# Four heads in one tile: exponentials, adds and masks of an attention step on Trainium2

## The chip, the cores and the metric

The kernel runs on one core of one Trainium2 chip. A core has five engines that run side by side, each with its own queue of instructions: TensorE (PE, matrix products; PEld are its weight loads), VectorE (DVE), ScalarE (ACT), GpSimd (POOL) and SyncE (SP), which here only issues transfers. PE writes to PSUM; the other data lie in SBUF, and the inputs and outputs in HBM. Instructions wait for each other by semaphores.

The metric is the device time of one execution in microseconds (us). Before the change it is 2343.66 us, the median of three runs (2343.58 to 2346.75).

## The reference, cut to what matters

The program computes one transformer block with conditioning, on x of 2 x 2048 x 512 in float32: 16 heads of 32, causal attention, and an MLP of 2048.

```
qkv = (xm @ Wqkv) -> q, k, v            # 2 batches, 16 heads, 2048 tokens, 32 per head
scores = q k^T * hd ** -0.5, causal     # each query sees itself and what is before it
attn = softmax(scores)
out = attn v -> x + gate * (out @ Wproj + bproj)
h = gelu(norm(x) @ W1 + b1);  x + gate * (h @ W2 + b2)
```

The change lies in the softmax: the exponentials, their causal mask, and the sums over the keys by which the output is divided.

## The kernel before, in words

The block is computed in stages: the products for q, k and v of a batch, the attention of that batch (`attention_phase`, once for each batch), its projection, and the MLP at the end. The change touches `attention_phase` alone. In the profile it runs from about 210 to 745 us and from about 982 to 1518 us.

**Units and steps.** Heads go in groups of four (HC = 4), which fill the 128 partitions of a product's output. A unit is one group c (four of them) with one block i of 512 queries (four of them): 16 units to a batch, numbered u, in the order i = 0, 1, 2, 3 for the first group and 0, 2, 1, 3 for the others. A unit goes over its keys in steps of 128 keys: 4i steps with all 512 queries, then three steps at the diagonal. The first of these (step 4i) has one block of 128 x 128 on the diagonal at its start; the second (step 4i + 1, the "two-block step") holds two key tiles of 384 and 128 queries in one bank, so it has two diagonal blocks; the last has 256 queries and one diagonal block. A batch has 144 steps, the kernel 288.

**One step** (`scores_t`): for each of the four heads PE writes the scores of 128 keys by up to 512 queries into a PSUM bank `st` (first a product that subtracts each query's maximum, L614, then the scores, L622); ACT writes the exponentials to a tile `e` of SBUF (L630), one of 128 x 512 for each head; at the diagonal POOL sets what lies above the diagonal to zero with `affine_select` (L636), one for each head, which covers one or two blocks. Between the heads PE and DVE compute the row maxima of later units (`row.score`, L500 and L495).

**Two steps later** (LAG = 2) PE multiplies the values by the exponentials (`values`, `products`, tile `o`). The products of a two-block step are done tile by tile: the 384 queries of all four heads, then the 128 of all four.

**The sums over the keys** are products with ones (`row_sums`, tile `sm`). To make fewer of them, the exponentials of up to four full steps are first added elementwise into a tile `ee` for each head: `begin_chain` adds the first two steps, `add_to` each later one (L658), and the diagonal step 4i is added to the last chain. POOL does these adds, except in a batch's last unit (u = 15), where DVE does them. The product with ones follows four steps after the chain's last add was issued.

**Buffers.** `e` has 16 buffers of one head, that is four steps; `ee` has 8, that is two chains. An exponential waits until everything that reads the buffer's old content is done.

**Order.** Each engine works through its own instructions in the order in which the program issues them; `act` and `mm` keep that order. So a select stands in POOL's queue behind all adds issued before it. In the last unit `row.prepare` (L446) adds work for the projection: products of two SBUF tiles on DVE (L459, L467) and an add on POOL (L465). After a batch's last unit its sums go to HBM (`finish`, L684), are read back (`load_sums`, L373), inverted on DVE (L380), written and read again; POOL multiplies the attention's result by them (tile `at`, L1266), and PE projects it (`ps_o`). In that stretch SP also loads pieces of the MLP's weights (L1154), which POOL adds up (L1166).

Of the kernel before, what the change touches and what calls it, by code (L numbers as in the profile page):

```python
# [8 lines left out]
F32 = mybir.dt.float32  # L9
F32R = mybir.dt.float32r  # L10
BF16 = mybir.dt.bfloat16
AF = mybir.ActivationFunctionType
ALU = mybir.AluOpType
# [4 lines left out]
P = 128  # L18
# [3 lines left out]
QB = 512  # L22
# [5 lines left out]
def dit_block_kernel(  # L28
# [36 lines left out]
    nc = tc.nc  # L65
# [5 lines left out]
    HC = P // HD  # L71
    TQ = QB // P
# [1 line left out]
    MTT = MT // P  # L74
    NG = T // MT
    LAG = 2
    E_BUFS = 16
    EE_BUFS = 8
    AHEAD = 3

    const = ctx.enter_context(tc.tile_pool(name="const", bufs=1))
# [53 lines left out]
    first = const.tile([P, 1], F32, tag="first", name="first")  # L135
# [68 lines left out]
    def mm(*args, **kw):  # L204

        return tc.keep_in_program_order(nc.tensor.matmul(*args, **kw))  # L206

    def act(ins):

        return tc.keep_in_program_order(ins)  # L210
# [70 lines left out]
    units = []  # L281
# [298 lines left out]
    def attention_phase(row):  # L580
        b, vv, kst, qst = row.b, row.vv, row.kst, row.qst
        with pool(f"att{b}") as ap, pool(
# [6 lines left out]
            def scores_t(u, step, n):  # L589

                def st_bank():

                    n_bank[0] += u == len(units) - 1
                    if n_bank[0] % 6 >= HC:
                        return ps_sp.tile([P, QB], F32, tag="s", name="st")
                    return ps_stp.tile([P, QB], F32, tag="st", name="st")

                c, i = units[u]
                tiles = steps_of[u][step]
                q0 = tiles[0][1]
                w = sum(QB - q for _, q in tiles)
                sts, es = [], []  # L610
                for h in range(HC):
                    g = slice(h * HD, (h + 1) * HD)
                    st = st_bank()
                    mm(  # L614
                        st[:, :w], sel[g, :], fold[u % 2][g, q0 : q0 + w],
                        start=True, stop=False,
                    )
                    sts.append(st)
                for h in range(HC):
                    at = 0  # L620
                    for j, q in tiles:
                        mm(  # L622
                            sts[h][:, at : at + QB - q],
                            kst[c, j // TQ][:, h, j % TQ * P : (j % TQ + 1) * P],
                            qst[u][:, h, q:],
                            start=False, stop=at + QB - q == w,
                        )
                        at += QB - q
                    e = ap.tile([P, QB], F32, tag="e", name="e", bufs=E_BUFS)
                    act(nc.scalar.activation(e[:, :w], sts[h][:, :w], AF.Exp))  # L630
                    if tiles[0][0] >= i * TQ:

                        d = e.rearrange("p (t k) -> p t k", k=P)[:, 0 : TQ : TQ - 1, :]
                        d = d[:, : len(tiles), :]
                        act(
                            nc.gpsimd.affine_select(  # L636
                                d, d, pattern=[[0, len(tiles)], [1, P]],
                                compare_op=ALU.is_ge, fill=0.0,
                                base=0, channel_multiplier=-1,
                            )  # L640
                        )
                    es.append(e)
                    if h < 2 and n >= 3 or h >= HC - n and n < 3:
                        row.score(1)
                if n >= 3:
                    row.score(1, st_bank)
                    row.score(min(n, HC) - 3)
                return es, max(0, n - HC)

            def new_sums():  # L650
                return [
                    ap.tile([P, QB], F32, tag="ee", name="ee", bufs=EE_BUFS)
                    for _ in range(HC)
                ]

            def add(u, h, dst, x, y):
                engine = nc.vector if u == len(units) - 1 else nc.gpsimd
                act(engine.tensor_tensor(dst, x, y, ALU.add))  # L658

            def add_to(u, chain, es):  # L660
                for h in range(HC):
                    add(u, h, chain[h], chain[h], es[h])

            def begin_chain(u, es0, es1):
                chain = new_sums()
                for h in range(HC):
                    add(u, h, chain[h], es0[h], es1[h])
                return chain

            def products(dst, lhs, es, q0, at, first, last):  # L670
                for h in range(HC):
                    mm(
                        dst[h * HD : (h + 1) * HD, q0:], lhs(h),
                        es[h][:, at : at + QB - q0], start=first, stop=last,
                    )

            def finish(u, o, sm):
# [26 lines left out]
            for u, (c, i) in enumerate(units):  # L704
                for n, tiles in enumerate(steps_of[u]):
                    w = sum(QB - q for _, q in tiles)
# [3 lines left out]
            def due(u, step):  # L710

                rate, past = 0.0, weight[step]
                for v in range(u + 1, len(units)):

                    left = sum(weight[step : max(step + 1, starts[v] - 3)])
                    rate = max(rate, (cum[v] - row.spent) / left)
                return row.spent + rate * past

            for u, (c, i) in enumerate(units):
# [5 lines left out]
                for n_step, tiles in enumerate(steps_of[u]):  # L725
                    last = n_step == steps - 1
                    if n_step == 0:
# [5 lines left out]
                    n = row.count(  # L733
                        due(u, starts[u] + n_step) - QB // 2,
                        u + AHEAD - (n_step < 2 and u > 0),
                    )
                    if u == 0 and n_step < LAG:

                        n = max(n, HC)
                    es, rest = scores_t(u, n_step, n)  # L740
                    rest = len(row.todo) - rest
                    make_rows = False
# [14 lines left out]
                    def tile_by_tile(dst, lhs, es, tiles, first, last):  # L757
                        at = 0
                        for n, (j, q) in enumerate(tiles):
                            products(  # L760
                                dst, lambda h: lhs(j, h), es, q, at,
                                first and n == 0, last and n == len(tiles) - 1,
                            )
                            at += QB - q
# [15 lines left out]
                    if n_step < i * TQ:  # L780
                        k = n_step % TQ
                        if k == 0:
                            even = es
                        elif k == 1:
                            chain = begin_chain(u, even, es)
                        else:
                            add_to(u, chain, es)
                        if k == TQ - 1 and n_step + 1 < i * TQ:
                            sums_of, wait = (chain, False), 2
                    elif i and n_step == i * TQ:  # L790
                        add_to(u, chain, es)
                        sums_of, wait = (chain, False), 2
                    else:

                        sums_of, wait = (es, last, tiles), i > 0 and not last
# [478 lines left out]
    row = Row(0)  # L1274
    with pool("wada") as wp, pool("qkv0") as qp, pool("hl0") as hp, pool(
# [161 lines left out]
        pieces.done()  # L1437

    attention_phase(row)


    past, row = row, Row(1)
    with pool("qkv1") as qp, pool("ps_qkv1", bufs=6, space=PSUM) as ps_mm:
# [29 lines left out]
        with pool("hl1") as hp:  # L1473
# [17 lines left out]
            pieces.done()  # L1491

    attention_phase(row)
    ps_s_cm.__exit__(None, None, None)

# [541 lines left out]
```

## Time and profile before

| | |
|---|---|
| median of three runs | 2343.66 us (2343.58 to 2346.75) |
| the profiled execution | 2339.57 us |
| its span, first to last instruction | 2337.8 us |
| granted TensorE clock | 0.997 of full speed |
| instructions | 34364 |

How to read the lines that follow. The page gives the busy time of each engine with its share of the span and its count of instructions; then digits for 40 equal slices of the span, each the busy share of a slice in tenths; then the chain of work that ended last, in shares by engine. A line of the view of waits reads: who waited, for whom, us in total, how often, longest us. A line of the timeline reads: start in us, length in us, engine, source line, operation, tile written <- tiles read, shapes, how many such instructions are merged in it, and in brackets the engine's idle time before it and what ended that. A group reads: line, engine, operation, tiles, shapes, count, busy us and mean ns of one, idle us before it. A line that lists a source's instructions gives min/median/max ns. The ends of matmuls are modelled, so PE looks somewhat busier than it is.

### The profile page before, as it was taken

To read this page: it belongs to the slowest core of one execution; us is meant where nothing else is said; L and a number is where in the kernel's file an instruction comes from. 1 tells how busy PE (TensorE), PEld (TensorE's weight loads), DVE (VectorE), ACT (ScalarE), POOL (GpSimd) and SP (SyncE) were. 2 spreads that over 40 slices of the span, in tenths; PEclk is the share of its full clock that TensorE was granted. 3 is DMA by queue.
4 is the path that set the end of the run, shared out by engine and by line. 5 is a ranking of instruction groups with operands and counts; after the bars stand their busy time and mean duration, and the time that the engine had idled before them with its cause. 6 is when DMAs were issued, how large, how long until landed. Compare 5 with 4: busy or idle time off the path is not lost.

```text
span 2337.8 us, 34364 instructions
## 1 busy us (share of the span) xinstructions
PE 2272.5 (97%) x12033; PEld 1376.1 (59%) x12033; DVE 1432.3 (61%) x3025; ACT 1007.9 (43%) x1952; POOL 1119.2 (48%) x1261
## 2 busy tenths in 40 slices
PE   7999999999999999999999999999999999999998
PEld 5787445455544588754545554344585486487477
DVE  4677766767657657777576766562473383375356
ACT  4434555555555243355555555603323322332320
POOL 7153997988893692289888898450000000000000
PEclk9999999999999999999999999999999999999999
DMA  9887132231223796622324113263354254353433
GB/s 303 272 277 185 33 86 65 64 83 46 91 100 116 260 307 222 167 60 67 75 64 100 42 42 133 97 229 108 107 176 154 84 176 145 116 162 126 141 120 131
DMA packets 160518, 311.64 MB, mean 133 GB/s; under 512 B 16544, under 2 KB 48844, under 8 KB 158552
## 3 DMA queue, kind: packets, MB, share of 16 engines
q1 hardware_dynamic: 155488, 285.53, 40.5%
q0 software_dynamic: 4480, 23.36, 2.6%
q8 instruction: 95, 1.56, 0.3%
q14 instruction: 79, 0.65, 0.1%
q10 hardware_dynamic: 376, 0.55, 0.1%
HBM read 229.95 MB, written 87.29 MB: 136 GB/s over the span
## 4 chain that ended last, share of the span: by engine, by line
PE 83%; DVE 6%; POOL 6%; issue 2%; DMA 2%; ACT 1%; SPq 0%; DVEq 0%; POOLq 0%; ACTq 0%
PE ps_a L206 24%; PE st L206 15%; PE ps_b L206 12%; PE o L206 9%; PE s L206 7%; PE ps_c L206 6%; POOL ee L658 5%; PE sm L206 4%; PE ps_o L206 3%; DVE junk L495 2%; PE ps_xt L214 1%; DVE mx L500 1%; POOL e L636 1%; ACT e L630 1%; PE ps_o L214 1%
## 5 line engine op out<-in xcount | busy, mean ns | idle before, releaser
L630 ACT ACTIVATE e<-st 128x512 f32<-128x512 f32 (+1 forms) x1152 | 574.5, 578 | 413.6 <-PE st L206 380.0
L500 DVE TENSOR_REDUCE mx<-s 128x1 f32<-128x512 f32 x608 | 406.2, 686 | 223.1 <-PE s L206 221.8
L658 POOL TENSOR_TENSOR ee<-ee,e 128x512 f32<-128x512 f32 x424 | 529.1, 1293 | 3.5 <-ACT e L630 3.3
L206 PE MATMUL st<-qst,kst 128*128 128x512 f32 (+3 forms) x1280 | 410.6, 386 | 0.0
L206 PE MATMUL s<-kst,qst 128*128 128x512 f32 (+3 forms) x994 | 375.3, 402 | 6.0 <-DVE mx L500 3.1
L206 PE MATMUL ps_a<-sum,w 128*128 128x256 f32 (+1 forms) x1088 | 346.6, 454 | 0.0
L206 PE MATMUL o<-e,vv 128*32 128x512 f32 (+3 forms) x2560 | 310.2, 539 | 6.9 <-POOL e L636 6.7
L206 PEld LDWEIGHTS st<-qst,kst 128*128 128x128 f32 x1280 | 227.8, 188 | 117.6 <-issue 88.3
L206 PEld LDWEIGHTS ps_a<-sum,w 128*128 128x128 f32 x1088 | 206.4, 190 | 109.7 <-issue 91.3
L658 POOL TENSOR_TENSOR ee<-e 128x512 f32<-128x512 f32 x168 | 210.3, 1288 | 102.3 <-ACT e L630 100.6
L495 DVE CUSTOM_DVE_ANT_0 junk<-s,causal 128x128 bf16<-128x128 f32 (+3 forms) x386 | 188.5, 488 | 92.4 <-PE s L206 85.0
L206 PEld LDWEIGHTS s<-kst,qst 128*128 128x128 f32 x994 | 185.7, 188 | 55.5 <-DVE mx L500 20.5
L636 POOL TENSOR_SCALAR_AFFINE_SELECT e<-e 128x128 f32<-128x128 f32 (+1 forms) x384 | 123.6, 362 | 73.1 <-ACT e L630 70.8
L206 PEld LDWEIGHTS <-sel 32*128 32x128 bf16 x1152 | 29.5, 91 | 199.7 <-issue 199.7
L1616 DVE TENSOR_TENSOR h<-c,ps_b 128x512 f32<-128x512 f32 x32 | 22.0, 688 | 202.0 <-PE ps_b L206 202.0
L206 PE MATMUL st<-fold,sel 32*128 32x512 bf16 (+1 forms) x1152 | 127.9, 372 | 13.5 <-DVE mx L495 6.4
L206 PEld LDWEIGHTS o<-e,vv 128*32 128x32 f32 x2560 | 65.3, 108 | 112.4 <-issue 72.8
L1790 ACT ACTIVATE h<-h,cols 128x512 f32<-128x512 f32 x96 | 69.3, 722 | 120.5 <-DVE h L1616 120.5
L206 PE MATMUL ps_b<-sum,w 128*128 128x256 f32 (+1 forms) x384 | 120.6, 450 | 0.0
L500 DVE TENSOR_REDUCE mx<-st 128x1 f32<-128x512 f32 x160 | 109.4, 684 | 2.4 <-PE st L206 0.6
L985 POOL TENSOR_TENSOR lo<-lo,hi 128x512 fp32r<-128x512 f32 x32 | 40.7, 1274 | 130.4 <-ACT hi L983 124.1
L206 PE MATMUL st<-kst,qst 128*128 128x512 f32 (+3 forms) x286 | 98.0, 370 | 0.0
(210 smaller groups left out, 3113.9 us busy)
## 6 DMA issues: line engine op xcount, KB each, us to landing
kst<-k SPq DMA_DIRECT2D x128, 256.0 KB
qst<-q SPq DMA_DIRECT2D x128, 256.0 KB
w<-w1d SPq DMA_DIRECT2D x32, 896.0 KB
w<-w2d SPq DMA_DIRECT2D x28, 1024.0 KB
w<-w2d SPq DMA_DIRECT2D x28, 768.0 KB
q<-hi SPq DMA_DIRECT2D x32, 256.0 KB
q<-lo SPq DMA_DIRECT2D x32, 256.0 KB
k<-hi SPq DMA_DIRECT2D x32, 256.0 KB
```

The source lines that it names most:

```text
L206: return tc.keep_in_program_order(nc.tensor.matmul(*args, **kw))
L214: return tc.keep_in_program_order(nc.tensor.transpose(dst, src, ident[:n, :n]))
L495: nc.vector.tensor_tensor_reduce(junk[:, :w], x, causal[:, QB - w :], 1.0, MASKED, ALU.add, ALU.max, m,)
L500: nc.vector.tensor_reduce(m, x, axis=AX.X, op=ALU.max)
L630: act(nc.scalar.activation(e[:, :w], sts[h][:, :w], AF.Exp))
L636: nc.gpsimd.affine_select(d, d, pattern=[[0, len(tiles)], [1, P]], compare_op=ALU.is_ge, fill=0.0, base=0, channel_multiplier=-1,)
L658: act(engine.tensor_tensor(dst, x, y, ALU.add))
L985: engine.tensor_tensor(lo, d, hi.bitcast(F32), ALU.subtract)
L1616: act(nc.vector.tensor_tensor(dst, x, y, ALU.add))
L1790: nc.scalar.activation(d, ps, AF.Gelu, bias=col(r_b1 + half * HF + f, 1))
```

## The change

The four heads of a step share one tile `e` of 128 x 4 x 512, and the four heads of a chain one tile `ee` of that size. There are 4 and 2 buffers of them, the same memory as before. ACT still writes one exponential for each head. POOL adds all four heads in one operation of 128 x 2048. The selects of a step come after its four exponentials, one for each diagonal block with the four heads in it: one in a one-block step, two in a two-block step. DVE's adds in the last unit stay one for each head. Products read the head's part of the tile. In the built program the order of the instructions on PE and ACT is the same as before. On DVE one operation of the projection between the batches changes place with its neighbours. In SP's queue transfers change places in the projections behind each attention phase: behind the first, loads of weight pieces for the MLP (L1154) now stand after the results of the last unit (`finish`, L684 and L685), some of them after the loads of x too; behind the second, loads of x, stores of x1 and loads of the MLP's weights are interleaved in another way. Only the first exponential of a step waits for the tile `e` to come free, and it waits for the whole add of the step that held it before.

```diff
-    E_BUFS = 16
-    EE_BUFS = 8
+    E_BUFS = 4
+    EE_BUFS = 2
...
+                e4 = ap.tile([P, HC, QB], F32, tag="e", name="e", bufs=E_BUFS)
                 for h in range(HC):
...
-                    e = ap.tile([P, QB], F32, tag="e", name="e", bufs=E_BUFS)
-                    act(nc.scalar.activation(e[:, :w], sts[h][:, :w], AF.Exp))
-                    if tiles[0][0] >= i * TQ:
-
-                        d = e.rearrange("p (t k) -> p t k", k=P)[:, 0 : TQ : TQ - 1, :]
-                        d = d[:, : len(tiles), :]
+                    act(nc.scalar.activation(e4[:, h, :w], sts[h][:, :w], AF.Exp))
+                    if h < 2 and n >= 3 or h >= HC - n and n < 3:
+                        row.score(1)
+                if tiles[0][0] >= i * TQ:
+                    for n_t in range(len(tiles)):
+                        lo = n_t * (TQ - 1) * P
+                        d = e4[:, :, lo : lo + P]
                         act(
                             nc.gpsimd.affine_select(
-                                d, d, pattern=[[0, len(tiles)], [1, P]],
+                                d, d, pattern=[[0, HC], [1, P]],
                                 compare_op=ALU.is_ge, fill=0.0,
                                 base=0, channel_multiplier=-1,
                             )
                         )
-                    es.append(e)
-                    if h < 2 and n >= 3 or h >= HC - n and n < 3:
-                        row.score(1)
...
-            def add(u, h, dst, x, y):
-                engine = nc.vector if u == len(units) - 1 else nc.gpsimd
-                act(engine.tensor_tensor(dst, x, y, ALU.add))
+            def add(u, dst, x, y):
+                if u < len(units) - 1:
+                    act(nc.gpsimd.tensor_tensor(dst, x, y, ALU.add))
+                    return
+                for h in range(HC):
+                    act(nc.vector.tensor_tensor(dst[:, h], x[:, h], y[:, h], ALU.add))
 
             def add_to(u, chain, es):
-                for h in range(HC):
-                    add(u, h, chain[h], chain[h], es[h])
+                add(u, chain, chain, es)
 
             def begin_chain(u, es0, es1):
-                chain = new_sums()
-                for h in range(HC):
-                    add(u, h, chain[h], es0[h], es1[h])
+                chain = ap.tile([P, HC, QB], F32, tag="ee", name="ee", bufs=EE_BUFS)
+                add(u, chain, es0, es1)
                 return chain
...
-                        es[h][:, at : at + QB - q0], start=first, stop=last,
+                        es[:, h, at : at + QB - q0], start=first, stop=last,
```

More of the change, by code (lines that the diff above doesn't have):

```diff
@@ L609, in scores_t @@
                 w = sum(QB - q for _, q in tiles)
-                sts, es = [], []
+                sts = []
                 for h in range(HC):
@@ L647, in scores_t @@
                     row.score(min(n, HC) - 3)
[L648 to L654, printed above, removed]
-            def add(u, h, dst, x, y):
-                engine = nc.vector if u == len(units) - 1 else nc.gpsimd
-                act(engine.tensor_tensor(dst, x, y, ALU.add))
+                return e4, max(0, n - HC)
+            def add(u, dst, x, y):
[4 more added lines that the diff above has]
+                    act(nc.vector.tensor_tensor(dst[:, h], x[:, h], y[:, h], ALU.add))
             def add_to(u, chain, es):
-                for h in range(HC):
-                    add(u, h, chain[h], chain[h], es[h])
+                add(u, chain, chain, es)
             def begin_chain(u, es0, es1):
-                chain = new_sums()
-                for h in range(HC):
-                    add(u, h, chain[h], es0[h], es1[h])
+                chain = ap.tile([P, HC, QB], F32, tag="ee", name="ee", bufs=EE_BUFS)
+                add(u, chain, es0, es1)
                 return chain
```

## The prediction

> **What bounds the kernel now.** I read the page first: busy time, the busy slices, and the chain that ended last.
>
> ```profile
> span 2337.8 us, 34364 instructions
> PE 2272.5 (97%) x12033; PEld 1376.1 (59%) x12033; DVE 1432.3 (61%) x3025; ACT 1007.9 (43%) x1952; POOL 1119.2 (48%) x1261
> POOL 7153997988893692289888898450000000000000
> PE 83%; DVE 6%; POOL 6%; issue 2%; DMA 2%; ACT 1%; SPq 0%; DVEq 0%; POOLq 0%; ACTq 0%
> ```
>
> TensorE (PE) bounds the kernel: 97% busy and 83% of the chain. GpSimd (POOL) is at 48% overall, but at 80 to 90% in the slices of the two attention phases, and idle in the last third. So its work matters only where PE waits for it. The view of waits says where that is:
>
> ```profile
> PEld o L206 <- POOL e L636: 27.3, 67, 1.6
> ```
>
> The weight loads of the value products wait for the masking selects (L636), 67 times, 27.3 us together. Hardly anything of PE waits for the adds (L658); but the selects stand behind the adds in POOL's queue. The timeline of one unit with i=3 shows it: POOL, ACT and PE from 325 to 352 us, with an undisturbed two-block step (291.97) for comparison.
>
> ```profile
> 326.52 5.01 POOL L658 TENSOR_TENSOR ee<-e 128x512 f32<-128x512 f32 x4 [1.00 <-ACT e L630]
> 331.47 9.96 POOL L658 TENSOR_TENSOR ee<-ee,e 128x512 f32<-128x512 f32 x8
> 341.37 1.07 POOL L636 TENSOR_SCALAR_AFFINE_SELECT e<-e 128x128 f32<-128x128 f32 x4
> 342.38 5.02 POOL L658 TENSOR_TENSOR ee<-ee,e 128x512 f32<-128x512 f32 x4
> 347.33 3.50 POOL L636 TENSOR_SCALAR_AFFINE_SELECT e<-e 128x256 f32<-128x256 f32 x12
> 325.84 2.06 ACT L630 ACTIVATE e<-st 128x512 f32<-128x512 f32 x4 [1.29 <-PE st L206]
> 341.31 2.06 ACT L630 ACTIVATE e<-st 128x512 f32<-128x512 f32 x4 [2.32 <-PE st L206]
> 350.82 2.06 ACT L630 ACTIVATE e<-st 128x512 f32<-128x512 f32 x4 [2.49 <-PE st L206]
> 345.67 1.20 PE L206 MATMUL st<-qst,kst 128*128 128x512 f32 x4
> 291.97 1.07 PE L206 MATMUL o<-e,vv 128*32 128x384 f32 x16
> 347.81 2.13 PE L206 MATMUL o<-e,vv 128*32 128x384 f32 x16 [0.95 <-POOL e L636]
> ```
>
> The exponentials of the two-block step are ready at 343.37 (341.31 + 2.06), but POOL has 16 adds in a row before them and reaches their selects at 347.33, 4 us late. PE stands idle for 0.95 us, and its 16 products then take 2.13 instead of 1.07 us, since they follow the four selects head by head. This place costs PE 0.95 + 1.06 = 2.0 us. The same step in the other units, by the PE timeline:
>
> ```profile
> 399.84 2.13 PE L206 MATMUL o<-e,vv 128*32 128x384 f32 x16 [0.32 <-POOL e L636]
> 535.46 2.13 PE L206 MATMUL o<-e,vv 128*32 128x384 f32 x16
> 672.30 2.13 PE L206 MATMUL o<-e,vv 128*32 128x384 f32 x16 [0.36 <-POOL e L636]
> 697.23 2.13 PE L206 MATMUL o<-e,vv 128*32 128x384 f32 x16 [1.20 <-POOL e L636]
> 739.04 2.49 PE L206 MATMUL o<-e,vv 128*32 128x384 f32 x11 [0.67 <-POOL e L636]
> 1121.64 2.13 PE L206 MATMUL o<-e,vv 128*32 128x384 f32 x16 [0.65 <-POOL e L636]
> 1173.63 2.13 PE L206 MATMUL o<-e,vv 128*32 128x384 f32 x16 [0.18 <-POOL e L636]
> 1309.48 2.12 PE L206 MATMUL o<-e,vv 128*32 128x384 f32 x16
> 1446.34 2.13 PE L206 MATMUL o<-e,vv 128*32 128x384 f32 x16 [0.48 <-POOL e L636]
> 1471.27 2.13 PE L206 MATMUL o<-e,vv 128*32 128x384 f32 x16 [1.20 <-POOL e L636]
> 1513.09 2.49 PE L206 MATMUL o<-e,vv 128*32 128x384 f32 x11 [0.67 <-POOL e L636]
> ```
>
> With idle time and length over 1.07 counted alike, the 12 places of these fences lose 20 us. That is all the change can win back: 0.9% of the span.
>
> **The adds.** 592 POOL adds of one head become 148 of four heads. Their length comes from POOL's TENSOR_TENSOR by size: min, median, max of a line, and the mean of a form.
>
> ```profile
> L1166 POOL TENSOR_TENSOR qst<-qst x40: 445/726/1065, 50.3 to 878.4; 128x256 f32<-128x256 f32 x24, 128x128 f32<-128x128 f32 x16
> L867 POOL TENSOR_TENSOR wqk<-wqk x17: 720/732/2370, 19.1 to 798.7; 128x256 f32<-128x256 f32 x16, 128x1024 f32<-128x1024 f32 x1
> L658 POOL TENSOR_TENSOR ee<-ee,e x424: 1252/1291/1356, 231.2 to 1469.6; 128x512 f32<-128x512 f32 x142
> L636 POOL TENSOR_SCALAR_AFFINE_SELECT e<-e 128x128 f32<-128x128 f32 x256 | 73.4, 324 | 63.8 <-ACT e L630 63.5
> L636 POOL TENSOR_SCALAR_AFFINE_SELECT e<-e 128x256 f32<-128x256 f32 x128 | 51.7, 439 | 9.3 <-ACT e L630 7.4
> ```
>
> The smallest values are 445 ns (128 elements), 720 (256), 1252 (512) and 2370 (1024). The slope from 256 to 512 continued to 2048 gives 1252 + 1536 x 2.08 = 4444 ns, that from 512 to 1024 gives 2370 + 1024 x 2.18 = 4606 ns. Eight adds now start over 9.90 us (331.47 to 341.37), so four take 4.95. An add in a chain will depend on the add right before it, where now three others lie between; I allow 0.05 us for that and take 4.55, a saving of 0.40 a step. Bounds: 4.44, and 4.95 + 0.1 = 5.05 (nothing saved, and a bubble). The Trainium skill, GPSIMD Engine Reference, section "Elementwise — side-by-side cycle accounting", gives 4497 ns for an fp32 add of 2048 elements; no run shown here has that size, and with that figure the saving would be 0.45 and the sum about 1 us better.
>
> The price of it: the add starts when the fourth head's exponential is done, not the first's. Where POOL was waiting (326.52), that is 325.84 + 2.06 = 327.90 and a little, 1.45 us later; where POOL is behind, nothing.
>
> **The selects.** 384 become 128. One more block of 128 costs 439 - 324 = 115 ns, so four blocks take 324 + 3 x 115 = 669 ns, and about 0.63 in a row, as four of 324 take 1.01 (341.37 to 342.38). A one-block step saves 0.38. A two-block step takes 2 x 0.63 = 1.26 against 4 x 0.36 = 1.44 (439 less the same overlap); and the products of the first block of all four heads need the first of these alone, so PE no longer steps from head to head.
>
> **Place by place.** At 326.52 the stretch begins 1.45 late; four adds and one select give back 4 x 0.40 + 0.38 = 1.98: the two-block selects start 0.53 earlier, at 346.80, and end at 347.43 and 348.06. PE is free at 346.87 (345.67 + 1.20). It loses 0.6 us in place of 2.0; its sister at 1121.64 is alike: together 2.7 us won. The places at 399.84, 535.46, 672.30, 1173.63, 1309.48 and 1446.34 close units with i=2, seven steps of adds behind one start, the first of them here:
>
> ```profile
> 363.59 5.02 POOL L658 TENSOR_TENSOR ee<-e 128x512 f32<-128x512 f32 x4 [6.89 <-ACT e L630]
> ```
>
> There 7 x 0.40 + 0.38 - 1.45 = 1.73 us earlier is more than any idle time in these rows; idle (1.34 in all) and stretch (6 x 1.06) go: 7.7 us. At 697.23 and 1471.27 (i=1) there are four adds, the second of which waits for its own fourth head as well; the selects come at about the old time, the 1.20 stays and most of the stretch goes: 2 x 0.85 = 1.7.
>
> In each batch's last unit the adds are on VectorE (DVE), and DVE and POOL visibly hold each other up:
>
> ```profile
> 734.88 3.84 DVE L658 TENSOR_TENSOR ee<-ee,e 128x512 f32<-128x512 f32 x4 [0.18 <-POOL e L636]
> 738.13 2.84 POOL L636 TENSOR_SCALAR_AFFINE_SELECT e<-e 128x256 f32<-128x256 f32 x4
> ```
>
> Four selects take 2.84 us instead of 1.44, each held by a DVE operation. Two selects in their place can be held at most twice. Of the 0.67 + 1.42 lost at 739.04 and at 1513.09 I take half, 1.0 each; bounds 0 and 2.1.
>
> **Queues.** In the built program SP's queue changes behind the first batch's attention: four loads of weight pieces (L1154) that stood before the storing of the last unit's sums now stand behind it, and four more that stood before the reading of the sums stand behind that. SP, PE and POOL there:
>
> ```profile
> 749.37 1.92 SPq L1154 DMA_DIRECT2D qst<-in_L_cond_W_dram  x4
> 751.85 0.53 SPq L684 DMA_DIRECT2D sum<-sums  x1
> 754.62 0.35 SPq L373 DMA_DIRECT2D r<-sum  x1
> 777.58 1.12 PE L206 MATMUL ps_o<-kst,at 128*128 128x512 f32 x2 [1.81 <-POOL at L1266]
> 840.16 1.75 POOL L1166 TENSOR_TENSOR vv<-vv 128x512 f32<-128x512 f32 x1
> ```
>
> The sums no longer wait for four issues (1.92 us) ahead of them, and their reading, at 754.62, for four more. What is made of them, POOL's product `at`, holds PE for 1.81 us at 777.58. Of that I take half, 1.0; bounds 0 and 1.8. The pieces that go to `vv` come later, past the loads of x; they are used at 840.16, more than 50 us on. Between the second attention and the MLP, loads of x and of MLP weights change places as well; PE has no idle row there that hangs on them, and I cost it at nothing, with 2 us to either side.
>
> Sum: 2.7 + 7.7 + 1.7 + 2.0 + 1.0 = 15 us.
>
> **What is costed at nothing.** The tiles of four heads come free as one: the first exponential of a step waits until the whole add of the step four before is done. That add ended at 342.38 + 5.02 = 347.40 and will end at 346.8; the exponential starts at 350.82. A margin of 4 us covers it; were it gone, ACT would be late, and PE behind it, by what the add is late. The one-block selects end later for the first head, but their products stand two steps on, and the products of the sums four. Order and number of operations on PE and ACT stay; on DVE one operation changes place with its neighbours in the projection between the batches.
>
> So the profiled execution would go from 2339.57 to about 2324.6 us (its span is 2337.8, with 1.8 around it). It was 4.1 us faster than the median of the runs, 2343.66; from the median the forecast is **2328 us** (rounded down).
>
> **Rivals.**
> - *The four-head add saves nothing* (5.05 us): slower. The late start of 1.45 stays and 0.1 is added per step: at the six places 1.45 + 0.7 - 0.38 = 1.8 later, 11 us in all; at the other four about 1.5, 6 us; four i=3 units whose two-block step has no row above, since it is hardly stretched now, lose about 1 each (estimate); less some 5 us for stretches that still go. +16 us: 2360. It decides from about 4.8 per add, where seven savings (7 x 0.15) no longer make up for 1.45 - 0.38. For it: every add then follows its own predecessor; against it: the four sizes lie on one line with a fixed part of about 0.18 (1252 - 512 x 2.1).
> - *The next wait takes over*: PE goes on earlier and meets DVE's maxima or ACT. Half the gain, -7: 2336. Against it: POOL apart, these engines are at 61 and 43%, and ACT's waits above are for PE.
> - *More than counted*: all 20 us go, and gaps that the modelled ends of PE hide: -24: 2320. For it: the 27.3 us on the weight loads.
> - *A four-head select costs like four*, and so does not do what it says: two-block steps need 2.0 us instead of 1.44; -8: 2336.
>
> **How the numbers follow.** Forecast 0.58, the add that saves nothing 0.15, next wait 0.14, more than counted 0.08, select like four 0.05. I call 0.2% (4.7 us) the bound of no change. Faster: 0.56 + 0.08 + 0.09 + 0.03 = 0.76; within: 0.02 + 0.05 + 0.02 + 0.02 = 0.11; slower: 0.13, all from the first rival. The range 2318 to 2346 leaves out that rival (0.13) and a little below.
>
> **What would show it.** Right: POOL's adds at 4.45 to 4.65 us and x148; selects at 0.6 to 0.7 us, x128; the two-block rows above at 1.07 to 1.5 us with no idle before them in the i=2 units; PEld's wait for the selects down from 27.3 us to under 10; ACT without a new wait for POOL. Wrong: adds over 4.8 us, ACT waiting for the adds, or stalls gone with the span unmoved.

## The result, and the profile after

The changed kernel takes 2325.97 us (median of four runs, 2324.34 to 2329.6) against 2343.62 for the kernel before on the same chip (2339.29 to 2346.75): ratio 0.9928, 95% interval 0.9915 to 0.994, 17.65 us faster. The profiled execution took 2326.19 us.

The page of the changed kernel: span, busy time, POOL's busy slices, the chain.

```profile
span 2324.4 us, 32565 instructions
PE 2263.0 (97%) x12033; PEld 1369.5 (59%) x12033; DVE 1435.5 (62%) x3025; ACT 1005.7 (43%) x1952; POOL 1020.5 (44%) x561
POOL 7152887877792692278777788340000000000000
PE 88%; DVE 5%; POOL 3%; ACT 1%; issue 1%; DMA 1%; SPq 0%; DVEq 0%; ACTq 0%; POOLq 0%
```

PE has as many instructions as before, POOL 561 in place of 1261 and 99 us less busy time, and POOL's share of the chain falls from 6 to 3%. Where that comes from, in the groups of costliest instructions:

```profile
L651 POOL TENSOR_TENSOR ee<-ee,e 128x2048 f32<-128x2048 f32 x106 | 485.8, 4583 | 16.4 <-ACT e L630 9.1
L651 POOL TENSOR_TENSOR ee<-e 128x2048 f32<-128x2048 f32 x42 | 192.4, 4580 | 152.9 <-ACT e L630 152.9
L638 POOL TENSOR_SCALAR_AFFINE_SELECT e<-e 128x512 f32<-128x512 f32 x128 | 81.5, 658 | 94.3 <-ACT e L630 91.7 <-DMA kst<-k 2.6
```

148 adds of 4.58 us and 128 selects of 0.66 us. And in the view of waits:

```profile
PEld o L206 <- POOL e L638: 12.4, 24, 1.9
ACT e L630 <- POOL ee L651: 8.8, 6, 2.2
```

The weight loads now wait 12.4 us for the selects, 24 times, where it was 27.3 us and 67 times. That ACT waits for an add is rare: six times. The unit with i=3 that the prediction follows, POOL's timeline:

```profile
330.82 4.58 POOL L651 TENSOR_TENSOR ee<-e 128x2048 f32<-128x2048 f32 x1 [2.05 <-ACT e L630]
335.48 9.23 POOL L651 TENSOR_TENSOR ee<-ee,e 128x2048 f32<-128x2048 f32 x2
344.65 0.66 POOL L638 TENSOR_SCALAR_AFFINE_SELECT e<-e 128x512 f32<-128x512 f32 x1
345.39 4.57 POOL L651 TENSOR_TENSOR ee<-ee,e 128x2048 f32<-128x2048 f32 x1
349.92 2.40 POOL L638 TENSOR_SCALAR_AFFINE_SELECT e<-e 128x512 f32<-128x512 f32 x4
```

The last row merges four selects; the first two are those of the two-block step. They still stand behind the add of 345.39. The two-block steps that lost time before, by PE's timeline (the columns are those of before):

```profile
350.60 1.07 PE L206 MATMUL o<-e,vv 128*32 128x384 f32 x16 [0.90 <-POOL e L638]
...
401.16 1.07 PE L206 MATMUL o<-e,vv 128*32 128x384 f32 x16
...
535.58 1.07 PE L206 MATMUL o<-e,vv 128*32 128x384 f32 x16
...
670.93 1.07 PE L206 MATMUL o<-e,vv 128*32 128x384 f32 x16
...
695.02 1.07 PE L206 MATMUL o<-e,vv 128*32 128x384 f32 x16 [1.45 <-POOL e L638]
...
1115.26 1.07 PE L206 MATMUL o<-e,vv 128*32 128x384 f32 x16 [0.87 <-POOL e L638]
...
1459.65 1.07 PE L206 MATMUL o<-e,vv 128*32 128x384 f32 x16 [1.44 <-POOL e L638]
```

The stretch to 2.13 us is gone everywhere. In units with i=2 (401.16, 535.58, 670.93 and their three sisters of the second batch) no idle time is left; at four places it stays.

**A common measure.** For the experiments I take two things from each trace. First, the loss at the two-block steps: for each of the 30 of units 0 to 14, the time from the start of the matmul ahead of the 16 products to the start of the last of them, less 1.12 us, which it takes, to within 0.02 us, in the kernels below wherever the selects come in time. Unit 3 is the first of a batch with i=3, the one that the prediction follows; the later units with i=3 are among the others. Second, the length of the attention: from the first exponential of unit 1 to that of unit 15, and from there to the last value product, in both batches (474.2 + 474.6 and 48.4 + 48.4 us before). The products come two steps late, so that unit 14's two-block step falls into the second stretch. Each ratio is to the kernel before on the same chip.

| kernel | median, us | ratio to before, 95% | loss at two-block steps (unit 3, i=2, unit 14, others) | units 1 to 14 | the rest |
|---|---|---|---|---|---|
| before | 2343 to 2344 | 1 | 18.4 (3.9, 8.4, 4.7, 1.5) | 0 | 0 |
| changed | 2325.97 | 0.9928 [0.9915, 0.994] | 5.0 (1.9, 0, 3.0, 0) | -11.9 | -3.7 |
| changed, again (e9) | 2323.47 | 0.9916 [0.9903, 0.9929] | 5.0 (1.9, 0, 3.0, 0) | -11.7 | -5.0 |
| e1: tile alone | 2342.79 | 0.9994 [0.9986, 1.0003] | 19.1 (4.1, 8.8, 4.7, 1.4) | -0.6 | 0 |
| e2: selects alone | 2325.59 | 0.9922 [0.991, 0.9934] | 6.5 (1.9, 2.1, 2.5, 0) | -10.6 | -5.6 |
| e3: adds alone | 2338.45 | 0.9979 [0.9969, 0.9989] | 15.1 (4.4, 3.5, 5.4, 1.7) | -5.3 | +0.8 |
| e4: selects, adds by two | 2325.25 | 0.9924 [0.9912, 0.9936] | 2.3 (0.6, 0, 1.7, 0) | -12.4 | -6.3 |
| e5: changed, POOL slowed | 2342.19 | 0.9994 [0.9985, 1.0003] | 18.7 (4.4, 8.0, 4.9, 1.4) | +0.1 | -3.1 |
| e6: changed, add deferred | 2321.96 | 0.9908 [0.9895, 0.9921] | 0 | -12.4 | -5.5 |
| e7: before, adds deferred | 2327.16 | 0.9936 [0.9923, 0.9948] | 0 | -11.0 | -4.1 |
| e8: selects alone, deferred | 2324.88 | 0.9921 [0.9908, 0.9935] | 0 | -12.4 | -4.7 |
| e10: e6 but for the last unit | 2321.01 | 0.9908 [0.9894, 0.9922] | 0 | -12.5 | -7.8 |
| e11: e8 but for the last unit | 2324.09 | 0.9918 [0.9906, 0.993] | 0 | -12.5 | -7.1 |
| e12: e7 but for the last unit | 2328.93 | 0.9939 [0.9925, 0.9954] | 0.1 | -11.1 | -4.5 |

The last two columns are microseconds against before. In the changed kernel they sum to -15.6, near the 17.65 of the medians; unit 0 and the stretches ahead of and between the attentions scatter by some microseconds from one execution to the next (see the end).

### The profile page after: what moved, and what is told of

Its sections match the earlier page's. It is cut to its first block, busy times and chain, and to the rows that moved or that the text cites. A ratio compares the mean times of both kernels' runs of the same rounds, so it can differ in the third digit from the quotient of the medians.

```text
span 2324.4 us, 32565 instructions
## 1 busy us (share of the span) xinstructions
PE 2263.0 (97%) x12033; PEld 1369.5 (59%) x12033; DVE 1435.5 (62%) x3025; ACT 1005.7 (43%) x1952; POOL 1020.5 (44%) x561
## 4 chain that ended last, share of the span: by engine, by line
PE 88%; DVE 5%; POOL 3%; ACT 1%; issue 1%; DMA 1%; SPq 0%; DVEq 0%; ACTq 0%; POOLq 0%
PE ps_a L206 24%; PE st L206 17%; PE ps_b L206 12%; PE o L206 9%; PE s L206 8%; PE ps_c L206 6%; PE ps_o L206 5%; PE sm L206 4%; POOL ee L651 3%; DVE junk L495 2%; PE ps_xt L214 1%; DVE mx L500 1%; ACT e L630 1%; PE ps_o L214 1%; POOL kst L1160 0%
## 5 line engine op out<-in xcount | busy, mean ns | idle before, releaser
L651 POOL TENSOR_TENSOR ee<-ee,e 128x2048 f32<-128x2048 f32 x106 | 485.8, 4583 | 16.4 <-ACT e L630 9.1
L206 PE MATMUL o<-e,vv 128*32 128x512 f32 (+3 forms) x2560 | 294.7, 540 | 4.7 <-POOL e L638 4.7
L651 POOL TENSOR_TENSOR ee<-e 128x2048 f32<-128x2048 f32 x42 | 192.4, 4580 | 152.9 <-ACT e L630 152.9
L638 POOL TENSOR_SCALAR_AFFINE_SELECT e<-e 128x512 f32<-128x512 f32 x128 | 81.5, 658 | 94.3 <-ACT e L630 91.7
L206 PEld LDWEIGHTS o<-e,vv 128*32 128x32 f32 x2560 | 58.4, 108 | 100.6 <-issue 77.7
```

Source lines behind the costliest of these rows:

```text
L638: nc.gpsimd.affine_select(d, d, pattern=[[0, HC], [1, P]], compare_op=ALU.is_ge, fill=0.0, base=0, channel_multiplier=-1,)
L651: act(nc.gpsimd.tensor_tensor(dst, x, y, ALU.add))
```

## The experiments

**e1, e2, e3, e4: the parts apart.** All four have the four-head tiles. In e1 and e3 the select of each head is issued behind its exponential, as before; SP's order is then exactly that of before. In e1, e2 and e4 the adds are cut, in e4 as shown, in e1 and e2 with 1 in place of the 2:

```diff
-                    act(nc.gpsimd.tensor_tensor(dst, x, y, ALU.add))
...
+                engine = nc.vector if u == len(units) - 1 else nc.gpsimd
+                n = 1 if u == len(units) - 1 else 2
+                for h in range(0, HC, n):
+                    g = slice(h, h + n)
+                    act(engine.tensor_tensor(dst[:, g], x[:, g], y[:, g], ALU.add))
```

and in e1 and e3 the select goes into the loop over heads:

```diff
                     act(nc.scalar.activation(e4[:, h, :w], sts[h][:, :w], AF.Exp))
+                    if tiles[0][0] >= i * TQ:
+                        d = e4[:, h].rearrange("p (t k) -> p t k", k=P)
+                        d = d[:, 0 : TQ : TQ - 1, :][:, : len(tiles), :]
...
+                                d, d, pattern=[[0, len(tiles)], [1, P]],
```

> Four-head tiles as in the changed kernel, but four adds of one head and one select per head, behind each head's exponential, as before. Theory (the gain comes from POOL reaching the two-block selects earlier, and from one select serving all heads): nothing is won, because POOL's queue is the one of before; 2343.6 us, 2341 to 2346, against 2343.6 for the kernel before; adds still follow each other every 1.24 us, the 16 products of the two-block steps still take 2.13 us in units with i=2, PE's weight loads still wait some 27 us for the selects. Rival (the gain lies in the tiles: fewer tiles, fewer waits, release of four heads at once, other order on SP): most of the 17.7 us is there, under 2332.

Measured: 2342.79 us, no change. Two of its two-block steps in PE's timeline, one with i=3 and one with i=2, are those of the kernel before:

```profile
347.68 2.13 PE L206 MATMUL o<-e,vv 128*32 128x384 f32 x16 [0.95 <-POOL e L635]
...
399.68 2.12 PE L206 MATMUL o<-e,vv 128*32 128x384 f32 x16 [0.29 <-POOL e L635]
```

The tiles, their release and the number of buffers bring nothing and cost nothing.

> Selects of four heads as in the changed kernel, adds of one head, four a step (4.95 us a step instead of 4.58). Replaying POOL's queue with the durations of the profiles against fixed times of ACT and PE gives PE losses at the selects of 13.3 us for the kernel before, 5.1 here, 3.9 for the changed kernel (units 0 to 14 of both batches); the last units and the transition between the batches, 5.25 us in the changed kernel, should come with the selects. Theory: 8.2 + 5.25 = 13.5 us won, 2330, 2327 to 2334. Rival (the shorter adds carry the gain): under 6 us won, over 2338.

Measured: 2325.59 us, all of what the whole change brings, and below the range that I gave. My replay had 8.2 us won at the two-block steps (13.3 before, 5.1 left), where the measure above finds 11.9 (18.4 and 6.5): it counted too little loss before. PE's timeline of e2, the same two steps and unit 14's:

```profile
347.83 1.07 PE L206 MATMUL o<-e,vv 128*32 128x384 f32 x16 [0.90 <-POOL e L638]
...
398.71 1.07 PE L206 MATMUL o<-e,vv 128*32 128x384 f32 x16 [0.24 <-POOL e L638]
...
692.53 1.07 PE L206 MATMUL o<-e,vv 128*32 128x384 f32 x16 [1.16 <-POOL e L638]
```

With one select for four heads the stretch goes at once, though POOL's adds are as slow as before. Idle time is left in the i=2 unit too (0.24), and at unit 14 it is 0.29 us shorter than in the changed kernel (1.16 against 1.45).

> One add of four heads as in the changed kernel, selects of one head behind each head's exponential, as before. The same replay gives 7.3 us of PE loss against 13.3 before, 6.0 won; SP's order between the batches is the one of before, and the last units are as before, so nothing there. Theory: 2337.6, 2334 to 2341; in units with i=2 no idle time is left, in units with i=3 and i=1 (unit 14) PE still goes head by head. Rival (the shorter adds carry the gain): over 12 us, under 2332. Rival (the late start of 1.45 us eats the saving): 2343 or more.

Measured: 2338.45 us, as expected: 5 us won. The replay behind it was off, though: it had 7.3 us of loss left, where the measure finds 15.1. POOL's timeline of a unit with i=2, then PE's of the three steps:

```profile
364.35 4.58 POOL L650 TENSOR_TENSOR ee<-e 128x2048 f32<-128x2048 f32 x1 [8.44 <-ACT e L630]
369.00 9.26 POOL L650 TENSOR_TENSOR ee<-ee,e 128x2048 f32<-128x2048 f32 x2
...
397.72 2.48 POOL L635 TENSOR_SCALAR_AFFINE_SELECT e<-e 128x256 f32<-128x256 f32 x8
```

```profile
347.09 2.13 PE L206 MATMUL o<-e,vv 128*32 128x384 f32 x16 [1.07 <-POOL e L635]
...
398.72 1.59 PE L206 MATMUL o<-e,vv 128*32 128x384 f32 x16
...
694.06 2.13 PE L206 MATMUL o<-e,vv 128*32 128x384 f32 x16 [1.60 <-POOL e L635]
```

The selects at the same place in the kernel before:

```profile
399.32 2.54 POOL L636 TENSOR_SCALAR_AFFINE_SELECT e<-e 128x256 f32<-128x256 f32 x8
```

From the first add of that unit (364.35, before 363.59) to its two-block selects it is 33.37 us in place of 35.73. The first add waits longer (8.44 us for 6.89): that is the late start. In the i=2 units the saving of seven steps outweighs it, and the loss falls from 8.4 to 3.5; where only four steps of adds run without a pause it does not, and the loss grows: 3.9 to 4.4 at unit 3, 4.7 to 5.4 at unit 14. So the long add gives with one hand and takes with the other.

> Selects of four heads, adds of two heads, two a step: about 2 x 2.36 = 4.72 us a step, but the first starts when the second head's exponential is done, about 1 us before the fourth's. Replay: 2.3 us of PE loss against 3.9 for the changed kernel. Theory (what counts is when POOL reaches the selects): 2324.4, 1.6 us below the changed kernel's 2326.0, 2322 to 2327. Rival (what counts is the number of POOL's instructions and their summed time): between the selects alone and the changed kernel, 2327 to 2330.

Measured: 2325.25 us; from the changed kernel, not resolved by the times. In the trace the expected 1.6 us is there and more: a loss of 2.3 us against 5.0. The three steps in PE's timeline of e4:

```profile
347.03 1.07 PE L206 MATMUL o<-e,vv 128*32 128x384 f32 x16 [0.23 <-POOL e L638]
...
397.79 1.07 PE L206 MATMUL o<-e,vv 128*32 128x384 f32 x16
...
691.07 1.07 PE L206 MATMUL o<-e,vv 128*32 128x384 f32 x16 [0.78 <-POOL e L638]
```

0.23 and 0.78 us in place of 0.90 and 1.45, at twice as many adds and 19 us more busy time of POOL (1039.4 against 1020.5): for the loss, when POOL gets there counts, not how much it does.

**e5: the rival that saves nothing.** One more operation on POOL behind every add, with a result that nobody reads:

```diff
+    spare = const.tile([P, P], F32, tag="spare", name="spare")
...
                     act(nc.gpsimd.tensor_tensor(dst, x, y, ALU.add))
+                    act(nc.gpsimd.tensor_tensor(spare, ident, ident, ALU.add))
```

> The changed kernel with one more GpSimd operation behind every four-head add: an add of 128 x 128 values that nobody reads (445 ns alone, about 0.40 in a row), so that a step of adds costs about 4.98 us, as four single adds do, and still starts at the fourth head's exponential. The result is unchanged. This is the prediction's first rival, that the four-head add saves nothing. The prediction counted it 16 us above the kernel before, 2360. Replay of POOL's queue: 22.8 us of PE loss against 13.3 before and 3.9 for the changed kernel, so 19 us above the changed kernel, 2345, 2340 to 2352. If POOL's lateness does not matter (the gain comes from the form of the select alone): 2326 to 2329.

Measured: 2342.19 us, 16 above the changed kernel and level with the one before. POOL's timeline of e5 at the i=3 unit, and the line of its view of waits:

```profile
338.83 4.55 POOL L652 TENSOR_TENSOR ee<-ee,e 128x2048 f32<-128x2048 f32 x1
343.35 0.40 POOL L653 TENSOR_TENSOR spare<-ident 128x128 f32<-128x128 f32 x1
343.70 0.63 POOL L639 TENSOR_SCALAR_AFFINE_SELECT e<-e 128x512 f32<-128x512 f32 x1
```

```profile
PEld o L207 <- POOL e L639: 34.4, 38, 2.8
```

A step of adds takes 343.70 - 338.83 = 4.87 us, and by the medians 0.3 us a step more than in the changed kernel costs all that it won; in the trace 3.0 us of it are left in the attention, all in the last units. The break-even lies near there, at about 4.9 us a step. An add that saves nothing, 4.95 us a step and more, was not run. Nearly all the loss is idle time; from the first to the last product the 30 steps take 24.1 us together, 23.9 in the changed kernel and 36.0 before. The two-block step behind those rows:

```profile
349.97 1.39 PE L207 MATMUL o<-e,vv 128*32 128x384 f32 x16 [2.05 <-POOL e L639]
```

**e6, e7, e8: the adds behind the selects.** The diagonal step's add is issued one step later, so that POOL meets the selects of the two-block step first:

```diff
-            pending = []
+            pending, late = [], []
...
+                    while late:
+                        add_to(*late.pop())
...
                     elif i and n_step == i * TQ:
-                        add_to(u, chain, es)
+                        late.append((u, chain, es))
```

e6 does this to the changed kernel, e7 to the kernel before, with nothing merged, e8 to e2.

> The changed kernel with the four-head add of each unit's diagonal step issued one step later, behind the selects of the two-block step and not ahead of them. Theory (the stalls that are left, 0.90, 1.45, 0.87 and 1.44 us, come from selects that stand behind that add): all four go, the 16 products of the two-block steps follow without idle time, 4.7 us won, 2321.5, 2319 to 2324; ACT gets no new wait, its margin shrinks from 3.5 to 1.5 us. Rival (the deferred add meets the next wait, the release of the exponentials' tile or SP's other order between the batches): 2326 or more.

> The kernel before, four adds and four selects a step, with the four adds of each unit's diagonal step issued one step later, behind the selects of the two-block step. No operation is merged. Theory (what PE loses is the lateness of the selects, and POOL's order decides it): idle time and head-by-head stretch go in all units but the last of each batch, 13.3 us by the replay, 16 by the rows: 2329, 2326 to 2332, most of what the change won without its change. Rival (one select for four heads is needed, since PE otherwise goes head by head): under 8 us, 2336 or more.

> Selects of four heads, adds of one head (four a step, 4.95 us), and the diagonal step's adds deferred as in the run beside it. Theory (adds matter only through the selects that stand behind them): with the selects in front, merged or single adds make no difference: within 1.5 us of the run with merged adds deferred, 2321.5, 2319.5 to 2324. Rival (shorter adds help by themselves, by releasing tiles sooner): 2 us or more slower than it.

Measured: 2321.96, 2327.16 and 2324.88 us. In all three the loss at the 30 steps is nil. At unit 3 of e7, a row of POOL and one of PE (the first merges the four selects of step 4i and the four of the two-block step):

```profile
340.97 2.50 POOL L636 TENSOR_SCALAR_AFFINE_SELECT e<-e 128x128 f32<-128x128 f32 x8
```

```profile
346.39 1.07 PE L206 MATMUL o<-e,vv 128*32 128x384 f32 x16
```

So e7 gets 16 of the change's 17.65 us without merging anything: the lateness of the selects is the cause, and POOL's order decides it. e6 came out as expected. e8 was 2.9 us slower than e6, where I expected 1.5 at most; their attentions differ by 0.8 us in the traces (-17.9 against -17.1). In e6 some of the gain was lost again in the last units, whose adds on DVE were deferred too: -5.5 us there, against -7.8 in e10, which leaves their order as it was.

**e9 to e12: the same, but for the last unit.** There the order stays, so that SP's order is also that of the kernel each is made from:

```diff
+                        if u < len(units) - 1:
+                            late.append((u, chain, es))
+                        else:
+                            add_to(u, chain, es)
```

> The changed kernel once more, so that the three others have it on the same chip: 2326.0, 2324.5 to 2327.5.

> The changed kernel with the diagonal step's add one step later in units 0 to 14 only; in each batch's last unit, whose adds are VectorE's, the order stays, and so does SP's order. Theory: the aligned starts of the steps gave 3.7 us at the four stalls that were left, and the last units lose nothing here: 3.7 under the changed kernel of this call, 2322.3, 2320.5 to 2324. Rival (what deferring won comes from SP's other order): within 1 us of the changed kernel.

> As the run before it, with adds of one head, four a step (4.95 us). Theory (adds matter only through the selects behind them): within 1 us of the deferred kernel with merged adds. Rival (shorter adds release the tiles sooner, which PE feels): 2 us or more slower than that.

> The kernel before, nothing merged, with the diagonal step's adds one step later in units 0 to 14 only; SP's order is the one of before. The two-block steps of units 0 to 14 lose nothing in either, so against the deferred kernel with merged operations this one lacks the last units' gain (1.0 us each by the aligned starts) and the other order on SP (0 to 2 us): 2 to 4 us slower than that, 2324.3 to 2326.3; within 0.5 us of it would say that neither the last units nor SP's order bring anything.

Measured: 2323.47, 2321.01, 2324.09 and 2328.93 us. The changed kernel came out 1 us below its expected range. e10 is 2.5 us under it in the medians, with intervals that overlap, and 3.6 us shorter in the attention of the traces (-20.3 against -16.7); its median is the lowest of all kernels run, though its ratio is that of e6. POOL's timeline of e10 at the i=3 unit, and PE's three steps:

```profile
343.61 0.63 POOL L638 TENSOR_SCALAR_AFFINE_SELECT e<-e 128x512 f32<-128x512 f32 x1
345.22 1.22 POOL L638 TENSOR_SCALAR_AFFINE_SELECT e<-e 128x512 f32<-128x512 f32 x2 [0.98 <-ACT e L630]
346.41 4.55 POOL L651 TENSOR_TENSOR ee<-ee,e 128x2048 f32<-128x2048 f32 x1
```

```profile
348.57 1.07 PE L206 MATMUL o<-e,vv 128*32 128x384 f32 x16
...
399.72 1.07 PE L206 MATMUL o<-e,vv 128*32 128x384 f32 x16
...
692.15 1.07 PE L206 MATMUL o<-e,vv 128*32 128x384 f32 x16
```

The two selects now wait 0.98 us for ACT, the add stands behind them, and PE does not wait at all. e12, with nothing merged, does the same in its two-block steps:

```profile
346.32 1.07 PE L206 MATMUL o<-e,vv 128*32 128x384 f32 x16
...
397.52 1.07 PE L206 MATMUL o<-e,vv 128*32 128x384 f32 x16
```

It has SP's order of before and is still 14.0 us faster than the kernel before on its chip (2342.92 us), so that the gain of POOL's order does not come from SP's. It is 7.9 us slower than e10, though, not 2 to 4; the traces show 4.7 of it in the attention, 3.3 of that in the last units, where the four-head selects help. The rest I could not place: the profiled execution of e12, 2324.4 us, was the fastest of its six.

e11 lies 3.1 us behind e10 and e8 2.9 behind e6, which is what the rival in both expectations had; the intervals overlap. The profiled executions of e11 and e10 differ by 3.4 us: 0.7 in the attention as measured above, 1.6 in unit 0 of the second batch, 1.2 between the batches. e8 and e6 have the same 1.6 us there. Unit 0 has i=0 and so no adds, and in the changed kernel itself its length differs by 1.6 us between two executions (see the end). So it is not shown that the shorter adds bring anything outside the attention.

## Why the prediction was right

The forecast, 2328 us, was 2 us above the result, and its reason holds: PE lost time where selects stood behind adds in POOL's queue, and the change brings them earlier and frees all heads at once. Point by point:

- *The add.* I took 4.55 us a step. Alone it takes 4.58, and two follow in 344.65 - 335.48 = 9.17, so 4.585 each: a saving of 0.37 for 0.40. The Trainium skill, GPSIMD Engine Reference, section "Elementwise — side-by-side cycle accounting", has 4497 ns; the trace shows some 85 ns more.
- *The select.* 658 ns for 669. It costs PE nothing more, and the rival in which it costs like four falls.
- *Units with i=3.* 2.7 us forecast, 3.9 - 1.9 = 2.0 measured: 0.90 and 0.87 us of idle time stay and not 0.6. From the first add to the two-block selects it is 349.92 - 330.82 = 19.10 us, for 20.81 before: 1.71 us saved and not 1.98.
- *Units with i=2.* 7.7 forecast, 8.4 measured, and no idle time left, as stated.
- *Units 14.* 1.7 forecast, 4.7 - 3.0 = 1.7 measured. Its idle time even grew from 1.20 to 1.45 us, by the late start.
- *Not counted:* 1.5 us at the smaller stretches of other units, all of it won.
- *Costed at nothing.* ACT's margin held: 8.8 us of waits for the adds against 10.9 before.
- *The next wait.* At the two-block steps 13.4 us went in units 0 to 14 and 5.7 in the last units; of these 19.1 the attention's length shows 15.6 (11.9 + 3.7). The 3.5 between are the part of that rival that is true.
- *The signs.* All came but one: PEld waits 12.4 us for the selects, not under 10. The four steps that keep their idle time hold 4.7 us of it.
- *The rival that saves nothing* was sized worst: 16 us over the kernel before by my count, level with it in e5, the nearest that was run. I took 5.05 us for the add, where e5 has 4.87, and let some 5 us of stretch go, where 36.0 - 24.1 = 11.9 went: the four-head select takes the stretch away however late it comes. Its point of decision, 4.8 us, was near: 4.9.

**Last units:** 2.0 us forecast. The two-block step itself won 2.8 us in each (from 4.01 to 1.18 us by the measure above, without the 1.12 taken off), but DVE's adds and the sums behind them gave some of it back, as a row of DVE and one of PE show:

```profile
732.00 5.55 DVE L654 TENSOR_TENSOR ee<-ee,e 128x512 f32<-128x512 f32 x4 [0.53 <-POOL e L638]
```

```profile
737.60 0.62 PE L206 MATMUL sm<-ee,ones 128*32 128x512 f32 x1 [0.64 <-DVE ee L654]
```

DVE's four adds, 3.84 us before, take 5.55, and a sum waits 0.64 us for them. Of the 3.7 us won from unit 15's first exponential on, 1.7 are unit 14's, so 2.0 are left: the forecast's size, though not by its working.

**SP's queue:** this step failed. I took 1.0 us for the sums that are stored and read sooner. They are, at 741.08 and 747.53 in SP's queue, eleven and seven us earlier than before, four of them because the attention ends sooner:

```profile
741.08 0.52 SPq L678 DMA_DIRECT2D sum<-sums  x1
745.10 1.92 SPq L1148 DMA_DIRECT2D qst<-in_L_cond_W_dram  x4
747.53 0.34 SPq L373 DMA_DIRECT2D r<-sum  x1
```

And PE's wait of 1.81 us for `at` is gone in every kernel with this order (the changed one twice, e2, e4, e5, e10, e11), while with the old order there (e1, e3, e7, e12) 1.2 to 2.0 us stay, and with a third order (e6, e8) 1.1 and 2.4; e12's line in the view of waits:

```profile
PE ps_o L206 <- POOL at L1271: 1.8, 1, 1.8
```

But the stage is not shorter for it. From the last value product of one batch to the first exponential of the next, the changed kernel is 1.5 us shorter than before, the same program run again 2.3 us longer, and the others with its order 0.6 to 4.9 us longer; with the old order it is between 0.5 us shorter and 2.4 longer. So no gain of the order shows in the stage. Where that time goes was not followed.

The nearness of the sum is in part luck: 1.5 us that were not counted and 0.7 too little at i=2 make up for 0.7 too much at unit 3 and for the 1.0 of SP's queue that no run shows.

What the sum hid is how the parts share it. I added the savings of adds and selects in one account. Alone, the selects win 17.9 us of median, the adds 5.0, both 17.65. Once the selects are merged the shorter adds change the loss only from 6.5 to 5.0 us: better by 2.1 at i=2, worse by 0.5 at unit 14, where the later start counts.

## What to carry to other kernels

When a fast consumer waits for a short operation, look at what stands ahead of it in its engine's in-order queue: issuing the long add after the short selects won 16 and 14 us (e7, e12) with no operation merged, most of what merging won. A merged operation starts when its last input is there; the merged add paid here only where a long unbroken run of savings followed the later start. So merge what the consumer is stepping through piece by piece (here the selects), and try middle sizes for the rest.

## What the runs showed that I had not expected

In the two profiled executions of the changed kernel units 1 to 14 agree within 0.2 us, but not what lies between the batches. The first exponential of the second batch stands at 976.29 and at 979.35 us, while the last products of the first batch end within a microsecond of each other:

```profile
976.29 2.07 ACT L630 ACTIVATE e<-st 128x512 f32<-128x512 f32 x4 [0.91 <-PE st L206]
```

```profile
979.35 2.06 ACT L630 ACTIVATE e<-st 128x512 f32<-128x512 f32 x4 [0.91 <-PE st L206]
```

The stretch from the last products to there differs by 3.9 us, a good part of what runs of one kernel scatter by (5.3 and 7.8 us for the changed kernel, up to 10.8 for e3). Unit 0, which the common measure leaves out, has two forms: in the first batch it takes 12.8 us from its first exponential to that of unit 1 in the one execution and 11.2 in the other, and every trace of this case has one of these two lengths in each batch. A gain of 2 or 3 us is therefore read better from aligned stretches than from medians of a few runs. The last unit has two forms as well: DVE's four adds take 5.55 us in the one execution and 4.44 in the other,

```profile
731.80 4.44 DVE L654 TENSOR_TENSOR ee<-ee,e 128x512 f32<-128x512 f32 x4 [0.53 <-POOL e L638]
```

and PE's wait of 0.64 us for the sums is there only in the first: 0.6 to 0.7 us per batch between executions of one program.
